# Layer 0's gate rows turned by way of DRAM and VectorE, two biases queued later, filler split between two places

## The chip, the core and the metric

The kernel runs on one core of a Trainium2 chip. The metric is device time in microseconds. TensorE (PE) multiplies matrices and loads their stationary operand (PEld), VectorE (DVE) and ScalarE (ACT) work on elements, GpSimd (POOL) does small elementwise work and issues indirect DMAs, SyncE (SP) issues most other DMAs. Each engine runs its own instructions in order and waits on semaphores.

## The reference

Two layers over N = 2708 rows of D = 256 features, in float32, with one adjacency matrix:

```python
def layernorm(x): return (x - mean(x)) / sqrt(var(x) + 1e-5)

# layer 0
n = layernorm(x)
s = where(adj > 0, (n @ Wq.T + bq) @ (n @ Wk.T + bk).T / 16, -9e15)
x = x + elu(softmax(s) @ (n @ Wv.T + bv))
n = layernorm(x)
# 8 experts, the best two per row, weights normalized over the two
xn = layernorm(n)
y_e = gelu((xn * ln_g[e] + ln_b[e]) @ W1[e] + b1[e]) @ W2[e] + b2[e]      # W1 256x1024
x = x + sum over the two of weight * y_e         # chosen by n @ Wr + br
# layer 1
h = layernorm(x) @ W_fc + b_fc
s = where(adj > 0, h @ w_att[:256] + (h @ w_att[256:]).T + b_att, -1e9)
x = x + softmax(s) @ h
n = layernorm(x)
x = x + sum over the best two of softmax weight * (gelu(n @ W1[e] + b1[e]) @ W2[e] + b2[e])   # W1 256x512
```

## The kernel before

**Tiles and blocks.** Rows are cut into 22 tiles of 128 (the last has 20 rows) and into six blocks of queries, five of four tiles and a last one of 148 rows. `layer0_attention` walks the blocks b and, inside each, the 22 key tiles k. At each k it makes scores (L545, PE), their exponential (L557, ACT), the product with the mask (L560, DVE; `p_last` in the last block), and, three steps later (LAG), the product with the values (L609, PE). The masks of the next block are made beside this: adjacency is loaded by SP (L394), compared (L411, DVE) and turned in 32 by 32 squares (L417, DVE). The experts' weights are copied into a packed layout in DRAM in the background, by SP (L1021 to L1034).

**Routing.** When a block ends, its four tiles are evicted (L634) and each becomes a generator, `finish`, that goes on into `Experts.route`. A `Line` starts a generator every third step (`gap`) and takes each running one a stage further at every k. In layer 0 a tile's route goes: statistics of the second layernorm (L251 to L257, the last on POOL); the row to `xd` in DRAM (L1120, SP), the normalized row `xn` and the twice normalized row for the experts (L261, DVE); the columns of `xn` for the gate by `to_columns`, which is two PE transposes (L274) and an ACT copy (L275) into `gT`; the gate product (L1156, PE) and its logits (L1160, DVE); the best two, their softmax (L1185, ACT), the place in the expert's region (L1188 to L1204); and two scatters of the row into `disp` (L1207, POOL). Once 16 tiles are routed, `begin` works out the first 24 slots (a slot is 128 rows of one expert) and fetches the first three, rows by SP (`fetch_rows`, L1388 to L1401: four quarters `xg` and the pair `who` of row number and weight), weights by POOL (`fetch_weights`, L1368, into a ring of four).

**Experts.** `slots` takes the slots one after the other. `turned` turns a slot's rows on DVE (L1436, then L1442 in layer 0); `up` makes the output bias times the row's weight (L1454 on DVE in layer 0, L1456 on ACT in layer 1) and the first product (L1463, PE) with gelu (L1471, ACT); `down` makes the second product (L1479, PE), the result `y` (L1485, DVE) and its scatter into `xd` (L1498 adds in layer 0, L1491 writes in layer 1). The products of neighbouring slots alternate on PE. SURE is 43 slots that there must be, SLOTS = 50 the most there can be. OFTEN = 45 slots run in a straight row; then every engine reads the number used (L1565), and each further slot stands in a nested `tc.If` (L1572). With these inputs layer 0 has 45 slots and layer 1 has 47. Weights are fetched three slots ahead, rows five, up to SLOTS.

**Layer 1's beginning.** `keys_and_values` puts PAUSE = 28 products that nobody reads on PE (`busy`, L914), loads the rows (L723) and norms them; the first use on PE is again a pair of transposes (L274).

**Order.** SP's order is the program's own throughout; so are those of PE, ACT and DVE in layer 1. In layer 0 the scheduler orders PE, ACT, DVE and POOL by its own estimates; `tc.issue_after(ins)` only says that an instruction comes behind `ins` on its engine.

Of the kernel before, what the change touches and what calls it, by code (L numbers as in the profile page):

```python
# [83 lines left out]

MASKS_AHEAD = 2

PAUSE = 28


FULL_AFTER = {14: 20, 16: 24}  # L90
# [2 lines left out]
SLOTS = (2 * N - E) // P + E  # L93
RING = 4

OFTEN = SURE + 2
AHEAD = 3
ROWS_AHEAD = 5
DROW = D + 2
# [5 lines left out]
def adj_ffn_kernel(ctx: ExitStack, tc: tile.TileContext, a: dict, out: bass.AP):  # L105
# [160 lines left out]
    def by_quarters(row):  # L266

        return row.rearrange("p (g c j) -> p g c j", g=GROUP, c=DC)

    def to_columns(dst, src, r):  # L270

        tp = misc.tile([P, GROUP, P], F32, name="misc")
        for c in range(DC):
            nc.tensor.transpose(tp[:, c, :r], src[:, c * P : (c + 1) * P], ident[:r, :r])  # L274
        nc.scalar.copy(dst, tp[:, :DC, :r])  # L275
# [77 lines left out]
    def layer0_attention(line):  # L353
        with ExitStack() as scope, ExitStack() as until_last:
# [18 lines left out]
            xin = {}  # L373

            def load_x(t):
                xin[t] = rows0.tile([P, D], F32, name="xin", bufs=9)
# [161 lines left out]
            def scores(b, k, g, apart, mT):  # L538
                b0, nb, ts_ = BLOCKS[b]
                kr, k0 = ROWS[k], k * P  # L540
                if k == NT - 1:
                    return tail_scores(b, g, apart, mT)
                ps = ps_s.tile([P, BN], F32, name="s")
                for c in range(DC):
                    nc.tensor.matmul(  # L545
                        ps[:kr, :nb], xnT[:, c, k0 : k0 + kr], g[:, c, :nb],
                        start=(c == 0), stop=(c == DC - 1 and k < KEYS),
                    )
                if k >= KEYS:
                    for j, t in enumerate(ts_):  # L550
                        r = ROWS[t]
                        nc.tensor.matmul(
                            ps[:kr, j * P : j * P + r], apart[:, j, :kr], minus_big[:, :r],
                            start=False, stop=(j == len(ts_) - 1),
                        )
                p = of_block(b, "p", [P, nb], F32, bufs=6)
                nc.scalar.activation(p[:kr, :nb], ps[:kr, :nb], AF.Exp, scale=1.0 / 16.0)  # L557
                mask = MASKS[b].of_key(mT, k)
                if k < KEYS:
                    nc.vector.scalar_tensor_tensor(  # L560
                        p, p, LARGEST, mask, op0=ALU.min, op1=ALU.mult
                    )
# [475 lines left out]
    class Experts:  # L1038
        def __init__(self, layer, hidden, packed_weights, w_gate, gate_bias, own_norm, xd, disp, early):
# [3 lines left out]
            self.seen = const.tile([P, E], BF16, name=f"seen{layer}")  # L1043
            nc.vector.memset(self.seen, 0.0)
            self.routed, self.begun, self.pads = 0, False, []
            self.written = []
            self.groups = [f"written{layer}", f"late{layer}", f"apart{layer}", f"after{layer}", f"rows{layer}"]
            self.early = early
# [55 lines left out]
        def route(self, t, x, logits=None):  # L1104
# [14 lines left out]
            if own_norm:  # L1119
                self.beside_early(nc.sync.dma_start(of_tile(xd, t), x[:r]))  # L1120

            if own_norm:
                xt = rows.tile([P, D], F32, name="xn", bufs=4)[:r]
                normed(xt, x[:r], mean, once)
                normed(by_quarters(rows2[:r, 0, :D]), in_chunks(x[:r]), mean, twice)
            else:
                row = normed(by_quarters(rows2[:r, 0, :D]), in_chunks(x[:r]), mean, once)
# [20 lines left out]
                )  # L1148
            lg = small.tile([P, E], F32, name="lg")
            if logits is None:  # L1150
                gT = routing.tile([P, DC, P], F32, name="gT", bufs=2)
                to_columns(gT[:, :, :r], xt, r)
                yield
                ps = misc.tile([P, GROUP, P], F32, name="misc").rearrange("p g n -> p (g n)")
                for c in range(DC):
                    nc.tensor.matmul(  # L1156
                        ps[:r, :E], gT[:, c, :r], w_gate[:, c, :],
                        start=(c == 0), stop=(c == DC - 1),
                    )
                nc.vector.tensor_add(lg[:r], ps[:r, :E], gate_bias[:r])  # L1160
            else:
                nc.vector.scalar_tensor_tensor(
                    lg[:r], logits, once, gate_bias[:r], op0=ALU.mult, op1=ALU.add
                )
# [201 lines left out]
        def fetch_weights(self, s, behind_add=None):  # L1366
            w, packed = self.ring[s % RING], self.packed_weights[0]
            start = nc.gpsimd.indirect_dma_start(  # L1368
                w, None, packed[:],
                bass.IndirectOffsetOnAxis(ap=self.weight_row[:, s : s + 1], axis=0),  # L1370
                bounds_check=E * P - 1, oob_is_err=False,
            )
            if behind_add is not None:
                tc.add_manual_dep(
                    start.ins, behind_add.ins.name,
                    mybir.DependencyInfo(
                        mybir.DependencyClass.Sync, mybir.DependencyReason.DATA
                    ),
                    reason="no sooner than the results",
                )  # L1380
            return w

        def fetch_rows(self, s):
# [41 lines left out]

        def slots(self, two, ps_mm, ps_acc, line):
            hidden, own_norm, xd = self.hidden, self.own_norm, self.xd
            _, hc, w2, b2, b1, ln, row = self.packed_weights

            def turned(s):  # L1430

                w, (xg, _) = self.weights[s], self.rows_[s]
                xe = two.tile([P, DC, P], F32, name="xe")
                raw = two.tile([P, DC, P], F32, name="xe_raw") if own_norm else xe
                with tc.issue_after(self.issued.ins) if own_norm and s < OFTEN else ExitStack():
                    nc.vector.transpose(  # L1436
                        raw.rearrange("p c (t i) -> p t c i", t=GROUP),
                        xg.rearrange("p t (c j) -> p t c j", c=DC),
                    )
# [9 lines left out]
            def up(w, xe, factor):  # L1449


                bias2 = two.tile([P, D], F32, name="bias2", bufs=2 if own_norm else 4)
                if own_norm:
                    nc.vector.tensor_scalar(bias2, w[:, b2:b1], factor, None, ALU.mult)  # L1454
# [21 lines left out]
            def down(s, w, who, hT, bias2, then):  # L1476
                ps = ps_acc.tile([P, D], F32, name="acc")
                for f in range(hc):
# [3 lines left out]
                    )  # L1482
                then()
                y = two.tile([P, D], F32, name="y", bufs=3)
                self.issued = nc.vector.scalar_tensor_tensor(  # L1485
                    y, ps, who[:, 1:2], bias2, op0=ALU.mult, op1=ALU.add
                )
                at = bass.IndirectOffsetOnAxis(ap=who.bitcast(I32)[:, 0:1], axis=0)
# [12 lines left out]
                if s < FULL_AFTER[self.early]:  # L1501
                    tc.declare_no_dep(start.ins, group=self.groups[3], reason="other rows of xd")
                    tc.add_to_no_dep_group(self.groups[2], start.ins)
                return start

            n = FULL_AFTER[self.early]
# [4 lines left out]
            def slot(s, s1):  # L1511
# [3 lines left out]
                    xe = turned(s)  # L1515

                after = turned(1) if s == 0 and not own_norm else None
                hT, bias2 = up(w, xe, who[:, 1:2])
                if s + 1 < s1 and not own_norm:
                    xe = after or turned(s + 1)  # L1520
                line.step()

                def fetch(behind_add=None):
# [30 lines left out]
            def in_a_row(s0, s1):  # L1554
# [6 lines left out]
                behind = None  # L1561


            in_a_row(0, OFTEN)
            used = nc.values_load(  # L1565
                self.used[0:1, 0:1], min_val=SURE, max_val=SLOTS,
                skip_runtime_bounds_check_because="a sum of rounded-up parts",
            )

            def others(s):  # L1570
                if s < SLOTS:
                    with tc.If(used > s):  # L1572
# [97 lines left out]
```

## Time and profile before

| | |
|---|---|
| median of 3 runs | 1231.23 us (1230.78 to 1231.45) |
| the profiled execution | 1228.5 us, its span 1226.7 us, mean granted TensorE clock 0.978 |
| TensorE matmul busy | 1150.6 us, 94% |
| VectorE, ScalarE, GpSimd busy | 565.7, 435.4, 421.3 us |
| layer 0: attention and experts | to about 510 us, and from there to 840 us |
| layer 1: attention and experts | from 847 us to about 1012 us, and from there to 1200 us |

A line of a group or of the timeline gives the engine, the line of the kernel, the operation, what it writes and reads, the shape and the count; in brackets stands the idle time before it and what ended it. A line of a stretch gives its length, the busy time of PE, PEld, DVE, ACT and POOL (each with its number of instructions), the granted clock, the share of the DMA engines and GB/s. A float32 product appears as two records, a transpose as one.

### The profile page before, as it was taken

To read this page: it belongs to the slowest core of one execution; us is meant where nothing else is said; L and a number is where in the kernel's file an instruction comes from. 1 tells how busy PE (TensorE), PEld (TensorE's weight loads), DVE (VectorE), ACT (ScalarE), POOL (GpSimd) and SP (SyncE) were. 2 spreads that over 40 slices of the span, in tenths; PEclk is the share of its full clock that TensorE was granted. 3 is DMA by queue.
4 is the path that set the end of the run, shared out by engine and by line. 5 is a ranking of instruction groups with operands and counts; after the bars stand their busy time and mean duration, and the time that the engine had idled before them with its cause. 6 is when DMAs were issued, how large, how long until landed. Compare 5 with 4: busy or idle time off the path is not lost. (4 is left out here: it accounts for less than half of the span.)

```text
span 1226.7 us, 20985 instructions
## 1 busy us (share of the span) xinstructions
PE 1150.6 (94%) x6528; PEld 928.7 (76%) x6528; DVE 565.7 (46%) x2147; ACT 435.4 (35%) x1254; POOL 421.3 (34%) x525
## 2 busy tenths in 40 slices
PE   8989999999998999789999999999999998999980
PEld 5656666666665675479999999997899977899880
DVE  5465663754546636352222222223866777422214
ACT  3222222222212212263233233232776757544330
POOL 3011020110211213053433343433654557655450
PEclk9999999999999999799999999999999999999996
DMA  9393973999988494538667966554001527655557
GB/s 205 59 178 69 197 163 101 211 197 235 227 175 202 104 211 193 175 63 258 168 183 207 344 155 176 128 169 105 8 1 41 206 58 202 186 155 141 143 184 278
DMA packets 206252, 198.17 MB, mean 162 GB/s; under 512 B 98027, under 2 KB 189636, under 8 KB 199992
## 3 DMA queue, kind: packets, MB, share of 16 engines
q1 hardware_dynamic: 178202, 110.45, 41.3%
q0 software_dynamic: 27040, 83.56, 21.6%
q10 hardware_dynamic: 894, 2.77, 0.6%
q8 instruction: 54, 0.88, 0.3%
q14 instruction: 62, 0.51, 0.1%
HBM read 263.92 MB, written 66.15 MB: 269 GB/s over the span
## 5 line engine op out<-in xcount | busy, mean ns | idle before, releaser
L1463 PEld LDWEIGHTS mm<-xe,ring 128*128 128x128 f32 x2192 | 261.9, 195 | 23.1 <-issue 7.0
L1463 PE MATMUL mm<-xe,ring 128*128 128x128 f32 x2192 | 267.5, 279 | 12.4 <-DMA ring<-L_ffn_packed,weight_row 4.7
L1479 PE MATMUL acc<-ring,hT 128*128 128x256 f32 x1096 | 255.0, 382 | 4.8 <-ACT hT L1471 4.8
L1471 ACT ACTIVATE hT<-mm,ring 128x128 f32<-128x128 f32 x548 | 156.8, 370 | 280.5 <-issue 156.9
L1479 PEld LDWEIGHTS acc<-ring,hT 128*128 128x128 f32 x1096 | 201.3, 191 | 29.8 <-ACT hT L1471 6.2
L609 PEld LDWEIGHTS acc<-v,p 128*128 128x128 f32 (+1 forms) x880 | 159.5, 190 | 65.7 <-issue 41.0
L609 PE MATMUL acc<-v,p 128*128 128x257 f32 (+1 forms) x880 | 204.1, 384 | 2.8 <-DVE p L560 1.8
L1485 DVE SCALAR_TENSOR_TENSOR y<-acc,who,bias 128x256 f32<-128x256 f32 x92 | 44.4, 483 | 345.6 <-PE acc L1479 337.6
L545 PE MATMUL s<-g,xnT 128*128 128x512 f32 x420 | 202.6, 602 | 0.0
L257 POOL TENSOR_TENSOR ln_rs<-ln_rs,minus_half 128x2 f32<-128x2 f32 x88 | 65.5, 748 | 266.0 <-DVE ln_rs L253 226.4
L1368 POOL DMA_INDIRECT ring<-L_ffn_packed,weight_row x98 | 103.6, 1057 | 145.7 <-PE acc L1479 107.1
L1207 POOL DMA_INDIRECT disp<-row,to x88 | 89.9, 1022 | 162.7 <-DVE to L1204 57.8
L854 PE MATMUL acc<-parts,m 128*128 128x266 f32 x924 | 127.7, 295 | 0.0
L557 ACT ACTIVATE p<-s 128x512 f32<-128x512 f32 x105 | 62.5, 596 | 180.5 <-PE s L545 146.1
L854 PEld LDWEIGHTS acc<-parts,m 128*128 128x128 f32 x924 | 118.3, 187 | 4.4 <-ACT raw L881 0.9
L545 PEld LDWEIGHTS s<-g,xnT 128*128 128x128 f32 x420 | 76.2, 192 | 53.7 <-issue 50.3
L560 DVE SCALAR_TENSOR_TENSOR p<-p,mT 128x512 f32<-128x512 f32 x100 | 68.3, 685 | 94.5 <-ACT p L557 94.4
L1498 POOL DMA_INDIRECT xd<-y,who x45 | 71.3, 1583 | 101.0 <-issue 59.2
L821 ACT CAST m<-mT 128x512 fp32r<-128x512 fp8e4 (+4 forms) x168 | 72.3, 475 | 11.2 <-PE acc L854 7.5
L1491 POOL DMA_INDIRECT xd<-y,who x47 | 47.0, 999 | 22.2 <-issue 11.6
L411 DVE TENSOR_SCALAR m_rows<-adj 128x512 fp8e4<-128x512 int32 (+1 forms) x105 | 42.1, 432 | 2.4 <-DMA adj<-in_adj_dram 2.4
L609 PE MATMUL acc<-v,p_last 128*128 128x257 f32 (+3 forms) x88 | 27.4, 413 | 8.8 <-DVE p_last L560 8.8
(251 smaller groups left out, 1040.8 us busy)
## 6 DMA issues: line engine op xcount, KB each, us to landing
adj<-in_adj_dram SPq DMA_DIRECT2D x100, 256.0 KB
L_ffn_packed<-in_L_ffn_W_dram SPq DMA_DIRECT2D x16, 1024.0 KB
xg<-disp SPq DMA_DIRECT2D x400, 32.0 KB
L_ffn_packed<-in_L_ffn_W_dram SPq DMA_DIRECT2D x16, 512.0 KB
neighbours<-mT SPq DMA_DIRECT2D x5, 1408.0 KB
mT<-neighbours SPq DMA_DIRECT2D x5, 1408.0 KB
xin<-in_x_dram SPq DMA_DIRECT2D x42, 128.0 KB
ring<-L_ffn_packed SPq DMA_DIRECT2D x4, 1154.0 KB
```

The source lines that it names most:

```text
L257: nc.gpsimd.tensor_tensor(rs[:r, 1], rs[:r, 0], minus_half[:r], ALU.pow)
L545: nc.tensor.matmul(ps[:kr, :nb], xnT[:, c, k0 : k0 + kr], g[:, c, :nb], start=(c == 0), stop=(c == DC - 1 and k < KEYS),)
L560: nc.vector.scalar_tensor_tensor(p, p, LARGEST, mask, op0=ALU.min, op1=ALU.mult)
L609: nc.tensor.matmul(accs[j][:r], p[keys, q0 : q0 + r], v[keys, k, :], start=(k == 0), stop=(k == NT - 1),)
L821: nc.scalar.copy(m[:, : q1 - q0], MASKS[b].of_key(mTs[b], k)[:, q0 - b * BN : q1 - b * BN],)
L854: nc.tensor.matmul(acc[:r], masks[t], parts[:, k, i], start=(k == 0 and i == 0), stop=False,)
L1207: nc.gpsimd.indirect_dma_start(disp[:], bass.IndirectOffsetOnAxis(ap=to[:r, j : j + 1], axis=0), rows2[:r, j], None,)
L1368: start = nc.gpsimd.indirect_dma_start(w, None, packed[:], bass.IndirectOffsetOnAxis(ap=self.weight_row[:, s : s + 1], axis=0), bounds_che ...
L1463: nc.tensor.matmul(ps[:, i, :], w[:, c * hidden + f * P : c * hidden + (f + 1) * P], xe[:, c, :], start=(c == 0), stop=(c == DC - 1),)
L1471: nc.scalar.activation(hT[:, f, :], ps[:, i, :], AF.Gelu, bias=w[:, b1 + f : b1 + f + 1])
L1479: nc.tensor.matmul(ps, hT[:, f, :], w[:, w2 + f * D : w2 + (f + 1) * D], start=(f == 0), stop=(f == hc - 1),)
L1498: start = nc.gpsimd.indirect_dma_start(xd[:], at, y, None, bounds_check=N - 1, oob_is_err=False, compute_op=ALU.add)
```

## The change

- The biases of layer 0's slots 0 and 1 are queued on DVE behind `self.issued`, which at that time is the first eviction copy of the last block.
- PAUSE goes from 28 to 12; 8 such products (BRIDGE) are put at the end of layer 0's row of slots.
- The row of slots is 45 long in layer 0, as before, and 47 in layer 1. Weights and rows are fetched up to that number and not beyond; a slot in a branch fetches its own. In layer 0 the number used is read behind the last scatter.
- For the 21 full tiles of layer 0, `xn` is written in feature quarters, stored to a scratch in DRAM, loaded back as four quarters on SP one stage later, and turned by one DVE transpose into `gT`, another stage later and behind the latest mask product or result. The tile of 20 rows keeps the PE transposes.

```diff
-PAUSE = 28
+PAUSE = 12
+BRIDGE = 8
...
-OFTEN = SURE + 2
...
+    def quarters(pool, name, src, bufs):
+
+        wide = D // GROUP
+        xq = pool.tile([P, GROUP, wide], F32, name=name, bufs=bufs)
+        for g in range(GROUP):
+            nc.sync.dma_start(
+                xq[g * QUARTER : (g + 1) * QUARTER],
+                src[:, g * wide : (g + 1) * wide].rearrange("(t i) e -> i t e", t=GROUP),
+            )
+        return xq
+
+    def turn(dst, xq):
+        return nc.vector.transpose(
+            dst.rearrange("p c (t i) -> p t c i", t=GROUP),
+            xq.rearrange("p t (c j) -> p t c j", c=DC),
+        )
...
# layer0_attention: mul_of = experts0.latest; scores():
-                    nc.vector.scalar_tensor_tensor(
+                    mul_of[0] = nc.vector.scalar_tensor_tensor(
                         p, p, LARGEST, mask, op0=ALU.min, op1=ALU.mult
                     )
...
# Experts.route:
+            turned = own_norm and r == P
             if own_norm:
                 xt = rows.tile([P, D], F32, name="xn", bufs=4)[:r]
-                normed(xt, x[:r], mean, once)
+                if turned:
+                    normed(by_quarters(xt), in_chunks(x), mean, once)
+                    scratch = dram.tile([P, D], F32, name=f"normed{t}")
+                    nc.sync.dma_start(scratch[:], xt)
+                else:
+                    normed(xt, x[:r], mean, once)
                 normed(by_quarters(rows2[:r, 0, :D]), in_chunks(x[:r]), mean, twice)
...
             if logits is None:
+                if turned:
+                    xq = quarters(rows0, "xq", scratch, 3)
+                    yield
                 gT = routing.tile([P, DC, P], F32, name="gT", bufs=2)
-                to_columns(gT[:, :, :r], xt, r)
+                if turned:
+                    with tc.issue_after(self.latest[0].ins) if self.latest[0] else ExitStack():
+                        turn(gT, xq)
+                else:
+                    to_columns(gT[:, :, :r], xt, r)
                 yield
...
# slots():
+            often = SURE + (2 if own_norm else 4)
...
                 if own_norm:
-                    nc.vector.tensor_scalar(bias2, w[:, b2:b1], factor, None, ALU.mult)
+                    with tc.issue_after(self.issued.ins) if gated else ExitStack():
+                        nc.vector.tensor_scalar(bias2, w[:, b2:b1], factor, None, ALU.mult)
...
-                self.issued = nc.vector.scalar_tensor_tensor(
+                self.issued = self.latest[0] = nc.vector.scalar_tensor_tensor(
                     y, ps, who[:, 1:2], bias2, op0=ALU.mult, op1=ALU.add
                 )
...
-                hT, bias2 = up(w, xe, who[:, 1:2])
+                hT, bias2 = up(w, xe, who[:, 1:2], own_norm and s < 2)
...
-                    if s + AHEAD < SLOTS and s + AHEAD == len(self.weights):
-                        self.weights.append(self.fetch_weights(s + AHEAD, behind_add))
+                    if len(self.weights) <= s + AHEAD < often:
+                        self.weights.append(self.fetch_weights(s + AHEAD))
                     for _ in range(2):
                         at = len(self.rows_)
-                        if at <= s + ROWS_AHEAD and at < (SLOTS if placed else n):
+                        if at <= s + ROWS_AHEAD and at < (often if placed else n):
                             self.rows_.append(self.fetch_rows(at))
...
-                elif own_norm and s == OFTEN - 1:
-
-                    added = down(*behind, lambda: None)
-                    fetch(added)
...
-            in_a_row(0, OFTEN)
-            used = nc.values_load(
-                self.used[0:1, 0:1], min_val=SURE, max_val=SLOTS,
-                skip_runtime_bounds_check_because="a sum of rounded-up parts",
-            )
+            in_a_row(0, often)
+            if own_norm:
+                idle = ps_mm.tile([P, GROUP, P], F32, name="mm").rearrange("p g n -> p (g n)")
+                for _ in range(BRIDGE):
+                    nc.tensor.matmul(idle[:, :D], ident, wfc[:, 0, :D], start=True, stop=True)
+            with tc.issue_after(self.last_start.ins) if own_norm else ExitStack():
+                used = nc.values_load(
+                    self.used[0:1, 0:1], min_val=SURE, max_val=SLOTS,
+                    skip_runtime_bounds_check_because="a sum of rounded-up parts",
+                )
 
             def others(s):
                 if s < SLOTS:
                     with tc.If(used > s):
+                        self.weights.append(self.fetch_weights(s))
+                        self.rows_.append(self.fetch_rows(s))
                         in_a_row(s, s + 1)
                         others(s + 1)
 
-            others(OFTEN)
+            others(often)
```

`to_columns`, `normed`, `by_quarters` and `in_chunks` stand as before; `turned` now calls `turn` for the same transpose it made itself.

More of the change, by code (lines that the diff above doesn't have):

```diff
@@ L372, in of_block @@
                 return pool.tile(shape, dtype, name=f"{name}_last", bufs=bufs)
-            xin = {}
+            xin, mul_of = {}, experts0.latest
             def load_x(t):
@@ L1045, in __init__ @@
             self.routed, self.begun, self.pads = 0, False, []
+            self.latest = [None]
             self.written = []
@@ L1364, in fill, with fetch_weights @@
                 yield
-        def fetch_weights(self, s, behind_add=None):
+        def fetch_weights(self, s):
             w, packed = self.ring[s % RING], self.packed_weights[0]
-            start = nc.gpsimd.indirect_dma_start(
+            nc.gpsimd.indirect_dma_start(
                 w, None, packed[:],
@@ L1372, in fetch_weights @@
             )
[L1373 to L1379, printed above, removed]
-                )
             return w
@@ L1434, in turned @@
                 raw = two.tile([P, DC, P], F32, name="xe_raw") if own_norm else xe
[L1435 to L1439, printed above, removed]
+                with tc.issue_after(self.issued.ins) if own_norm and s < often else ExitStack():
+                    turn(raw, xg)
                 if own_norm:
@@ L1447, in turned, with up @@
                 return xe
-            def up(w, xe, factor):
+            def up(w, xe, factor, gated):
                 bias2 = two.tile([P, D], F32, name="bias2", bufs=2 if own_norm else 4)
                 if own_norm:
-                    nc.vector.tensor_scalar(bias2, w[:, b2:b1], factor, None, ALU.mult)
+                    with tc.issue_after(self.issued.ins) if gated else ExitStack():
+                        nc.vector.tensor_scalar(bias2, w[:, b2:b1], factor, None, ALU.mult)
                 else:
@@ L1503, in down @@
                     tc.add_to_no_dep_group(self.groups[2], start.ins)
+                self.last_start = start
                 return start
@@ L1521, in slot, with fetch @@
                 line.step()
-                def fetch(behind_add=None):
+                def fetch():
                     for _ in range(2 if s + AHEAD < n else E):
@@ L1561, in in_a_row @@
                 behind = None
-            in_a_row(0, OFTEN)
-            used = nc.values_load(
-                self.used[0:1, 0:1], min_val=SURE, max_val=SLOTS,
-                skip_runtime_bounds_check_because="a sum of rounded-up parts",
-            )
+            in_a_row(0, often)
[8 more added lines that the diff above has]
+                )
             def others(s):
```

## The prediction

> **What bounds it now.** I read the page first: TensorE (PE) is busy nearly all the time, so a gain must come out of PE's own work or out of the few places where it stands still.
>
> ```profile
> PE 1150.6 (94%) x6528; PEld 928.7 (76%) x6528; DVE 565.7 (46%) x2147; ACT 435.4 (35%) x1254; POOL 421.3 (34%) x525
> ```
>
> Then busy time by stretch: layer 0's attention (to 510 us) and the experts after it. From 206 us PE is full and the DMA engines are full as well; in the last block, from 456 us, PE loses 9.2 of 54 us.
>
> ```profile
> 206.00:290.00 84.00, 84.00 (x336) 55.51 (x334) 44.63 (x164) 17.95 (x41) 12.84 (x21) 1.00 1.06 215
> ...
> 456.00:510.00 54.00, 44.80 (x224) 26.46 (x222) 24.53 (x124) 9.73 (x35) 12.99 (x18) 0.91 0.64 230
> ```
>
> The waits name that loss: VectorE (DVE) stands at slot 0's bias, whose rows have not landed, and the attention's mask product `p_last` is queued behind it.
>
> ```profile
> PE acc L609 <- DVE p_last L560: 8.8, 1, 8.8
> ...
> DVE bias L1454 <- DMA who<-disp: 13.0, 1, 13.0
> ```
>
> SyncE's (SP's) timeline shows why: slot 0's `who` is issued at 478.26 and the bias starts only at 497.57, 19.3 us later, while three weight gathers fill the DMA engines; rows for slot 2 take until 498.3, and only then come the row writes of tiles 17 to 19 (L1120).
>
> ```profile
> 478.26 0.40 SPq L1401 DMA_DIRECT2D who<-disp  x1
> ...
> 492.09 6.23 SPq L1395 DMA_DIRECT2D xg<-disp  x4
> ...
> 498.96 1.35 SPq L1120 DMA_DIRECT2D xd<-x  x3
> ```
>
> After the stall the granted clock is low for 5.5 us:
>
> ```profile
> 498.50:504.00 5.50, 5.47 (x14) 2.62 (x15) 1.53 (x7) 0.29 (x1) 2.11 (x4) 0.55 0.72 200
> ```
>
> Next the seam between the layers: last result (L1485), filler on PE (L914), a weight fetch that is not needed (L1368), the last scatter (L1498), the first row load, and layer 1's first transpose, which waits for the filler.
>
> ```profile
> 839.91 0.48 DVE L1485 SCALAR_TENSOR_TENSOR y<-acc,who,bias 128x256 f32<-128x256 f32 x1 [2.97 <-PE acc L1479]
> ...
> 841.49 12.32 PE L914 MATMUL acc<-wfc,ident 128*128 128x256 f32 x56 [1.62 <-DVEq L1572]
> 841.86 1.06 POOL L1368 DMA_INDIRECT ring<-L_ffn_packed,weight_row  x1 [3.08 <-PEq L1572]
> 843.22 1.57 POOL L1498 DMA_INDIRECT xd<-y,who  x1 [0.31 <-issue]
> ...
> 847.46 10.31 SPq L723 DMA_DIRECT2D kept<-xd  x22
> ...
> 853.65 0.38 PE L274 MATMUL misc<-ident,xn 128*128 128x128 f32 x2
> ```
>
> And layer 1's tail on PE: slots 45 and 46 run in branches, one after the other, with gaps.
>
> ```profile
> 1181.67 2.02 PE L1463 MATMUL mm<-xe,ring 128*128 128x128 f32 x16
> 1183.53 3.62 PE L1479 MATMUL acc<-ring,hT 128*128 128x256 f32 x16
> ...
> 1196.98 1.99 PE L1479 MATMUL acc<-ring,hT 128*128 128x256 f32 x8 [0.52 <-ACT hT L1471]
> ```
>
> **Part by part** (all against the profiled span of 1226.7 us).
>
> *Seam.* The last scatter has its row at 840.4 and needs the scatter before it to have landed; the wait on that ends at 841.1. Without L1368 and the register load ahead of it, it starts about 841.3 instead of 843.22, 1.9 us sooner, and with it the loads and the first `xn` (852.0 to 850.1). On PE 56 records took 12.32 us, 0.22 each. The bridge (16 records, 3.5 us) follows the last matmul at 839.87 directly, the branch costs about the 1.62 us it costs now, PAUSE 12 is 24 records, 5.3 us: PE is free at 850.3. The first transpose goes from 853.65 to 850.3: **-3.4** (-1.9 if filler is placed worse, -3.6 at best).
>
> Clock: the 1.62 us gap before L914 leaves the granted clock at 1.00 in the stretch after it, the 8.8 us stall brings 0.55; my gap stays at 1.6, so no price. The Trainium skill (TensorE: Matmul & The Clock Gate, Why this matters for your kernels) warns of idle gaps over about 3 us, after which the array runs at half clock; no row here lies between 1.6 and 8.8 us, and by the page a gap past 3 us would give back some 2 us as an estimate.
>
> *Tail.* Layer 1's straight row grows from 45 to 47 slots. A slot's period is 3.51 us (up starts at 1174.55 and 1178.07). From 1181.67, three ups and four downs back to back, as in the steady row, are 7 x 1.76 = 12.3, so PE ends at 1194.0 instead of 1198.97: **-4.9** (-3 if row loads come late). The unneeded fetches for slots 45 to 49 disappear from POOL and SP; they hid.
>
> *Transposes.* Each routed tile loses two on PE and a 371 ns copy on ScalarE. What PE gains is the step, not the 272 ns length:
>
> ```profile
> 407.80 0.42 PE L274 MATMUL misc<-ident,xn 128*128 128x128 f32 x2
> ...
> 408.05 1.88 PE L545 MATMUL s<-g,xnT 128*128 128x512 f32 x4
> ```
>
> 0.25 us per tile, 18 of the 21 full tiles inside the attention: **-4.5** (0 to -5.3). DVE gets 21 turns of 0.434 (L1436), 9.1 us in all; it is busy 5.3 tenths at 206 to 290, and PE takes a score's product three steps after it is made, about 10 us: 0.
>
> *The way through DRAM* adds on SP, per tile, one write and four loads, 105 issues of 0.32 to 0.6 us. The loads wait on SP for the write to land; behind them SP has adjacency, packing and, later, row loads. The turn sits in DVE's order, and the gate product L1156 in PE's, so both can hold up the attention. A 128 KB load with free engines is used 2.4 us after issue (847.46 to 849.85), the starved `who` 19.3 after; the round trip is two in series, 4.8 to 39 us. Hidden or not depends on where the scheduler puts the turn and L1156. In the present order it puts the mask turning late: adjacency loads issued from 224.5 are first used at 245.7, those from 264.7 at 302.9, and DVE waits 2.4 us in all at L411. It counts DMA on SP slower than it is, which leaves the turn late too. I take 0, the cover being those 20 to 38 us; uncovered, see the third rival.
>
> The Trainium skill (VectorE: DVE Perf Modes, Rules for kernel authors) speaks against the step: a 128x128 transpose belongs on TensorE if the result may be in PSUM. It also puts a DMA's fixed part near 2.0 us (DMA: Bandwidth & Descriptors, Anatomy of one DMA), which agrees with the 2.4 above. By that, two DMAs per tile, unhidden, would add 21 x 4 = 84 us; the sum above takes none of it.
>
> *Biases queued.* The biases of slots 0 and 1 go behind the first eviction copy (510.23 now), so the 8.8 us wait goes, and with it 0.45 x 5.5 = 2.5 us of low clock. Attention ends near 499; slot 0's `who` has landed at 497.5. I take **-10.5** (0 to -11.3). What could be late next is tile 17's turn: see the first rival.
>
> *Later routing.* If one more tile's softmax falls between gelus, it costs two table loads of 1283 ns: **+2.6** (0 to +7.7 for three). Three turns behind results in the expert stretch, where DVE's slack is a fraction of a us: **+0.9** (0 to +1.3).
>
> Sum: -3.4 -4.9 -4.5 -10.5 +2.6 +0.9 = -19.8. Span 1206.9; with the 1.8 around the span 1208.7; the median of the runs lies 2.7 above the profiled 1228.5: **1211.4 us**.
>
> **Rivals.**
> 1. *The stall moves to tile 17.* SP reaches its write at about 499, so its round trip ends at 504 to 505. If the scheduler put the turn inside the last block, DVE stands there as at the bias, and the -10.5 becomes 0 (up to +5, as 505 is later than 497.6): 1222, to 1227. For: the bias itself was placed 13 us too early, so its estimates can be short when gathers run. Against: tile 18's `xn` stands after the attention although its statistics were ready near 483, so a queue behind DMAs is counted as slow. Chance 0.22.
> 2. *Nothing moves by the DRAM way.* PE's 4.5 us are lost again to small waits of L1156 and the routing moves: 1216 to 1218, chance 0.1.
> 3. *Slower: L1156 waits in PE's order for the round trip.* Place: tiles 4 to 15, where the DMA share is 1.02 to 1.06 and SP stands in queue. The point where it decides is 20 us over 12 tiles, 1.7 us a tile; at 4.8 us a tile, one free round trip, it is +58; I price it at 3 us, +36: 1247. For: DMA is saturated there, every engine is in order. Against: the 20 to 38 us above. Chance 0.18.
>
> **How the numbers follow.** Forecast 0.5, rivals 0.22, 0.1, 0.18. The low end takes every best bound: -3.6 -5 -5.3 -11.3 = -25.2, 1206, and 3 us for an order that I can't see: 1203. The high end takes rival 1 whole and half of rival 3: 1240. 0.2% is 2.5 us, about what a measurement of this kernel can tell from no change. Slower by that: rival 3 (0.18). Same: a mild rival 3 or rival 1 at its worst (0.06). Faster: 0.76.
>
> **What would show it.** Right: no PE wait on `p_last` near 9 us; granted clock 1.00 through the last block; last scatter of layer 0 less than 2 us after its `y`; first layer 1 transpose some 10 us after that `y` instead of 13; ups and downs without gaps to the last slot; DVE waits at the new turn of under 5 us in all. Wrong: PE idle at L1156 or DVE idle at the turn with `xq` as releaser, in the blocks from 206 to 456 (rival 3) or once before the first expert (rival 1).

## Result, and the profile after

The changed kernel takes **1264.9 us** (median; 1264.0 to 1271.8) against 1231.3 us of the kernel before in the same comparison: ratio **1.028, interval 1.024 to 1.032**, slower by 34 us. The forecast was 1211.4, range to 1240: wrong in sign. The profiled execution took 1265.5 us, its span 1263.5.

First the page of the kernel after, the line of the engines' busy times. PE has less to do, 58 records fewer, and is still busy 2.6 us longer, over a span 37 us longer.

```profile
PE 1153.2 (91%) x6470; PEld 926.5 (73%) x6470; DVE 576.1 (46%) x2168; ACT 429.1 (34%) x1235; POOL 413.7 (33%) x519
```

Then busy time by stretch (length, busy us of PE, PEld, DVE, ACT and POOL, granted clock, DMA share, GB/s), the same two stretches as before:

```profile
206.00:290.00 84.00, 75.23 (x255) 46.87 (x254) 40.66 (x138) 15.71 (x33) 9.51 (x17) 0.94 0.90 200
...
456.00:510.00 54.00, 52.03 (x255) 34.71 (x254) 31.25 (x135) 11.02 (x35) 12.34 (x20) 0.97 0.63 162
```

The loss is where the kernel before was full: 8.8 us of PE in the first of them. The last block gained, but now ends at 530.1 us (510.7 before). The waits on PE name what is late:

```profile
PE mm L1485 <- DMA xg<-disp: 14.7, 1, 14.7
PE misc L1187 <- DVE gT L282: 10.9, 5, 3.5
PE misc L1219 <- DVE sel L1214: 6.3, 7, 1.1
...
PE misc L235 <- ACT gT L292: 5.2, 1, 5.2
```

The 8.8 us at `p_last` are gone. In their place stand the first slot's rows (L1485 is the first product of the experts), the gate product waiting for the new turn (L1187, L1156 before), the rank that follows it (L1219), and `fold_gate` (L235).

The timeline shows one of these places, the end of the third block:

```profile
299.07 0.51 PE L1187 MATMUL misc<-wr,gT 128*128 128x8 f32 x4
299.62 0.17 DVE L1191 TENSOR_TENSOR lg<-misc,L_ffn_br_b 128x8 f32<-128x8 f32 x1 [8.09 <-PE misc L1187]
...
300.72 0.17 PE L1219 MATMUL misc<-sel,before 128*128 128x8 bf16 x1 [1.14 <-DVE sel L1214]
...
303.52 0.61 DVE L434 STREAM_TRANSPOSE mT<-m_rows 128x128 int32<-128x128 int32 x2
...
303.99 0.40 DVE L282 STREAM_TRANSPOSE gT<-xq 128x256 f32<-128x256 f32 x1
304.45 1.02 PE L1187 MATMUL misc<-wr,gT 128*128 128x8 f32 x4 [3.53 <-DVE gT L282]
```

Two tiles' gate products stand next to each other in PE's order, with no score between them. VectorE waits 8.1 us for the first; only behind its logits, and behind mask work, comes the next tile's turn; for that PE waits 3.5 us. That tile's quarters had landed at 279.1, 25 us sooner; SP had issued their loads from 267.22 on:

```profile
267.22 8.28 SPq L275 DMA_DIRECT2D xq<-normed  x4
```

For tiles 4 to 11 the trace has 12 to 39 us between the last quarter's landing and the turn. Inside the gap the granted clock falls: it is 1.00 to 301.4, 0.50 from there to 311.7.

```profile
300.00:304.00 4.00, 0.19 (x2) 0.10 (x1) 3.79 (x20) 0.30 (x2) 1.30 (x2) 0.68 0.91 294
304.00:308.00 4.00, 2.41 (x8) 1.82 (x9) 2.50 (x16) 0.30 (x2) 0.65 (x1) 0.50 1.14 215
308.00:312.00 4.00, 4.00 (x6) 1.54 (x5) 0.00 (x0) 0.69 (x1) 1.92 (x2) 0.54 0.87 166
```

What runs there, most at 1061 ns a product instead of 592, is L546: the queries of the next block, without which no score of it can start. First their line after, then before (L529), where a score follows at once:

```profile
306.67 6.16 PE L546 MATMUL misc<-xnT,aT 128*128 128x512 f32 x8
```

```profile
268.21 3.60 PE L529 MATMUL misc<-xnT,aT 128*128 128x512 f32 x8
271.64 1.88 PE L545 MATMUL s<-g,xnT 128*128 128x512 f32 x4
```

From 120 to 560 us the granted clock is 0.94, against 0.98 before; this is part of why PE is busy longer with fewer records. In PE's order the queries now stand behind the last score of their block in four of five blocks; in the kernel before that was so in one, and in three they stood about four rounds of keys sooner.

SP's timeline for the first slots: `who` of slot 0 at 519.41 (478.26 before), and tile 17's row write behind twelve row loads, at 545.30.

```profile
519.41 0.46 SPq L1424 DMA_DIRECT2D who<-disp  x1
520.38 5.27 SPq L1418 DMA_DIRECT2D xg<-disp  x4
...
536.40 8.30 SPq L1418 DMA_DIRECT2D xg<-disp  x4
...
545.30 0.42 SPq L1138 DMA_DIRECT2D xd<-x  x1
```

The seam: the last scatter is 0.8 us behind its `y` (3.3 before), SP's loads 6.6 us (7.55 before), the first transposes 11.9 us (13.7 before).

```profile
876.74 0.48 DVE L1507 SCALAR_TENSOR_TENSOR y<-acc,who,bias 128x256 f32<-128x256 f32 x1 [6.54 <-PE acc L1501]
877.50 1.55 POOL L1520 DMA_INDIRECT xd<-y,who  x1 [5.48 <-DVE y L1507]
...
888.67 0.44 PE L291 MATMUL misc<-ident,xn 128*128 128x128 f32 x2 [0.53 <-DVE xn L261]
```

The tail on PE, straight now, waits for weights between the last slots:

```profile
1224.65 2.02 PE L1485 MATMUL mm<-xe,ring 128*128 128x128 f32 x16 [0.50 <-DMA ring<-L_ffn_packed,weight_row]
...
1229.45 2.02 PE L1485 MATMUL mm<-xe,ring 128*128 128x128 f32 x16 [1.05 <-DMA ring<-L_ffn_packed,weight_row]
```

From the layer-1 part's first transpose to its last result it is 346.8 us, 345.8 before. So nearly all of the loss is there by the first product of the experts, which starts 33 us later than before (544.8 against 511.8). From there on the results of the experts come 26 to 41 us later than before, the last 36.

### The profile page after: what moved, and what is told of

It is laid out like the page before. It is cut to its first block, busy times and chain, and to the rows that moved or that the text cites. A ratio compares the mean times of both kernels' runs of the same rounds, so it can differ in the third digit from the quotient of the medians.

```text
span 1263.5 us, 20873 instructions
## 1 busy us (share of the span) xinstructions
PE 1153.2 (91%) x6470; PEld 926.5 (73%) x6470; DVE 576.1 (46%) x2168; ACT 429.1 (34%) x1235; POOL 413.7 (33%) x519
## 5 line engine op out<-in xcount | busy, mean ns | idle before, releaser
L1485 PE MATMUL mm<-xe,ring 128*128 128x128 f32 x2192 | 266.7, 279 | 30.5 <-DMA xg<-disp 14.7
L1485 PEld LDWEIGHTS mm<-xe,ring 128*128 128x128 f32 x2192 | 262.4, 195 | 41.1 <-issue 25.3
L626 PE MATMUL acc<-v,p 128*128 128x257 f32 (+1 forms) x880 | 207.2, 386 | 3.7 <-ACT p L574 2.3
L1399 POOL DMA_INDIRECT ring<-L_ffn_packed,weight_row x92 | 97.3, 1057 | 120.4 <-PE acc L1501 78.0
L434 DVE STREAM_TRANSPOSE mT<-m_rows 128x128 int32<-128x128 int32 x100 | 33.1, 394 | 0.1
```

What stands on the lines that cost most here:

```text
L626: nc.tensor.matmul(accs[j][:r], p[keys, q0 : q0 + r], v[keys, k, :], start=(k == 0), stop=(k == NT - 1),)
L1399: nc.gpsimd.indirect_dma_start(w, None, packed[:], bass.IndirectOffsetOnAxis(ap=self.weight_row[:, s : s + 1], axis=0), bounds_check=E * P ...
L1485: nc.tensor.matmul(ps[:, i, :], w[:, c * hidden + f * P : c * hidden + (f + 1) * P], xe[:, c, :], start=(c == 0), stop=(c == DC - 1),)
```

## Experiments

The medians of the kernel before were 1227.9 us in the comparison of the first four runs, 1228.4 in the next four, 1229.1 and 1234.4 in the last two; so ratios are compared, and "us" of a difference is its ratio times 1231. "Attention ends" is the last product with the values in the profiled execution.

| run | time | ratio to before, interval | attention ends | first product of the experts |
|---|---|---|---|---|
| after | 1264.9 | 1.028 (1.024 to 1.032) | 530.1 | 544.8 |
| before | 1231.3 | 1 | 510.7 | 511.8 |
| no way | 1211.9 | 0.988 (0.985 to 0.990) | 499.9 | 500.8 |
| way only | 1268.9 | 1.033 (1.030 to 1.035) | 546.4 | 547.2 |
| trip unread | 1228.2 | 1.000 (0.998 to 1.001) | 506.1 | 519.9 |
| late by hand | 1215.0 | 0.989 (0.987 to 0.991) | 504.5 | 505.5 |
| queries first | 1254.0 | 1.021 (1.018 to 1.024) | 517.8 | 531.6 |
| turn later | 1246.7 | 1.014 (1.011 to 1.017) | 519.8 | 534.1 |
| one stage | 1215.0 | 0.989 (0.986 to 0.991) | 498.1 | 505.4 |
| no way, queries first | 1211.5 | 0.985 (0.982 to 0.988) | 499.9 | 500.9 |
| pinned 3 | 1257.1 | 1.022 (1.019 to 1.024) | 547.1 | 548.1 |
| pinned 2 | 1258.6 | 1.022 (1.020 to 1.025) | 551.4 | 552.3 |
| no landing wait | 1224.3 | 0.996 (0.994 to 0.998) | 505.6 | 514.9 |
| biases only | 1214.5 | 0.988 (0.985 to 0.990) | 499.3 | 500.3 |
| pinned, tiles 0 to 15 | 1236.6 | 1.002 (1.000 to 1.003) | 521.5 | 523.7 |
| way, tiles 0 to 15 | 1258.1 | 1.020 (1.018 to 1.021) | 532.0 | 545.5 |
| way, tiles 16 to 20 | 1226.7 | 0.993 (0.991 to 0.995) | 497.9 | 500.9 |
| trip on GpSimd | 1290.5 | 1.046 (1.044 to 1.048) | 557.9 | 558.9 |

### The way through DRAM taken out, and put in alone

```diff
-            turned = own_norm and r == P
+            turned = False
```

> The changed kernel with PE's transposes back for all tiles (no scratch, no quarters, no turn, no extra stage); biases, filler, straight rows and fetches as changed. In PE's order the gate products stand where they stood before (after 26, 29, 32, 35 rounds of keys, and so on). Theory A (the way through DRAM is the loss, because turn and gate product stand late in the order): 1209 to 1218 us, no PE wait at the gate product over 0.5 us. Theory B (SP's 105 more issues and their traffic are the loss): the same 1209 to 1218. Theory C (the loss is in the other parts, such as the later fetches or the queued biases): 1240 us or more.

1211.9 us, and no wait at the gate product. Theory C falls: the way through DRAM is the whole loss, 50 us (1.028 less 0.988), and the rest of the change is a gain of 15.

The opposite edit, the kernel before with `quarters`, `turn`, the scratch and the stage and nothing else:

> The kernel before with the way through DRAM alone. A and B: the seam is worth 1.8 us in the trace, the tail about 0, and the biases' gain is lost behind the later rows, so 1264 to 1272 us, with the first slot waiting for its rows some 10 to 15 us. C: 1229 to 1238 us.

1268.9 us, as expected. The first slot's late rows show at another place: VectorE stands 18.6 us at the first bias, ahead of the attention's last mask work, and PE 14.4 us at the products behind it, since this kernel does not queue the bias later.

### Transfers without the turn, lateness without transfers

In the first, the quarters are stored and loaded, and PE's transposes make `gT`:

```diff
-                    normed(by_quarters(xt), in_chunks(x), mean, once)
+                    normed(xt, x[:r], mean, once)
...
-                if turned:
-                    with tc.issue_after(self.latest[0].ins) if self.latest[0] else ExitStack():
-                        turn(gT, xq)
-                else:
+                if True:
                     to_columns(gT[:, :, :r], xt, r)
```

> The changed kernel with the scratch write, the four quarter loads and the extra stage kept, but nobody reads the quarters: PE's transposes make the columns. In PE's order the gate products stand one round of keys later than before (27, 30, 33, 36). A: within 5 us of the kernel without the way, 1210 to 1222 us. B: near the changed kernel, 1250 to 1268 us, SP still waiting some 40 us for the writes to land.

In the second, the kernel without the way gets ten idle stages:

```diff
-            turned = own_norm and r == P
+            turned = False
...
+                    if own_norm:
+                        for _ in range(10):
+                            yield
                     to_columns(gT[:, :, :r], xt, r)
```

> The kernel without the way through DRAM, with ten more stages put ahead of PE's transposes in layer 0's route: no scratch, no DMA more, only lateness. In PE's order the gate products stand 9 to 10 rounds later than before (36, 39, 42, 45; at the ends of the blocks 64, 64 and 86, 86). A: most of the loss comes back without any transfer, 1240 to 1265 us. B: 1209 to 1222 us.

The first, 1228.2 us, lies in neither theory's range: transfers and stage cost 16 us, more than A gave them and far less than B. The second, 1215.0, lies in B's range, and theory A falls with it: gate products ten rounds late cost nothing that the intervals tell (0.989 against 0.988). With unread quarters the loss is paid at the first slot's rows, where the kernel without the way has no such wait, and SP stands until writes have landed:

```profile
PE mm L1482 <- DMA xg<-disp: 13.8, 1, 13.8
```

```profile
SPq L275 <- DMA normed<-xn: 46.7, 14, 8.5
```

The row writes of tiles 4 to 7 (L1138) leave at 227.5, 244.5, 260.7 and 276.2 there, at 228.0, 240.8, 251.7 and 259.4 without the way: SP needs 16 us a tile instead of 10.5, and the program starts a tile every three rounds, 10.4 us. In the changed kernel they leave at 225.1, 243.5, 260.6 and 276.8. At these tiles SP is behind the program's pace, and the lag lasts: tile 15's row write leaves at 448.5 us with unread quarters and at 429.6 without the way, slot 0's row loads at 491.1 and 475.6.

### The extra stage, and SP's standing

One idle stage instead of ten, no transfers:

> The kernel without the way through DRAM, with one more stage ahead of PE's transposes: the stages of the run in which nobody read the quarters, without its transfers. Theory S (the 16 us of that run come from the stage, which sets the table of the first slots behind another tile's routing, so that slot 0's rows land late): 1222 to 1230 us with a wait for the first rows of 10 us or more. Theory T (they come from the transfers): 1210 to 1215 us, no such wait.

1215.0 us: theory T, at the edge of its range; PE stands 1.9 us before the first product, not 10. From here to the run with unread quarters, which has the same stages, the transfers cost 13 us (0.989 to 1.000).

Unread quarters again, but loaded from an older scratch, so that SP need not wait for a landing:

```diff
+                    earlier = self.stored[max(0, len(self.stored) - 5)]
...
-                    xq = quarters(rows0, "xq", scratch, 3)
+                    xq = quarters(rows0, "xq", earlier, 3)
```

> The run with unread quarters, its quarters now loaded from the scratch of the tile four before, so that SP need not stand until a write has landed: same issues, same bytes, same order on PE. Theory W (SP's standing, 47 us in 14 waits, made that run 13 us slower than the one with the stage alone): 1214 to 1220 us. Theory I (its issues and bytes did): 1224 to 1230 us.

1224.3 us, in theory I's range: 4.5 less by ratio, with intervals that touch. If that holds, a third of the 13 goes with SP's standing. But SP is hardly sooner for it: its pace at tiles 4 to 7 is 15 us, tile 15's row write leaves at 448.1 us and slot 0's loads at 490.0. So most of SP's lag is its issues, their bytes, and its waits for earlier DMAs of its own (16 us at L275 between 206 and 400 us); it stays open how these share it.

### Why late is dear only in the changed kernel

The gate product, `fold_gate` and the queries take turns in a PSUM pool of two banks (the ring), in the order of the program. Lateness by hand moves the gate product behind the queries in the program too. The scheduler's lateness does not: the queries, traced at round 16 of a block, must wait for banks that late gate products of earlier rounds hold. Two edits free them. One traces the queries at round 5:

```diff
-                    if k == NT - 6 and b + 1 < len(BLOCKS):
+                    if k == 5 and b + 1 < len(BLOCKS):
```

> The changed kernel, way through DRAM and all, but each next block's queries are traced at round 5 of a block instead of round 16, ahead of the block's gate products in the two-bank ring of PSUM that both use. The gate products stand as late in PE's order as in the changed kernel (28, 33.5, 39, 44; 58.5, 64, 64, 67.5), the queries at 25, 47, 69, 91 instead of 44, 64, 86, 108. Theory E (late gate products hold the next block's queries in the ring, and PE has no scores left at a block's end): attention ends 20 us sooner or more, near 505 to 512 us, and the time is 1232 to 1247 us. Theory D (the gate products themselves wait for the late turn on VectorE, wherever the queries stand): saves under 8 us, 1256 to 1265 us.

The other puts the turn eight more stages later:

```diff
                     xq = quarters(rows0, "xq", scratch, 3)
-                    yield
+                    for _ in range(8):
+                        yield
```

> The changed kernel with the turn eight stages later in the program, about where the scheduler put it of itself; the gate products stand as late or later (34, 37, 40, 44; 59, 64, 64, 67.5), but the queries, traced before them now, stand at 36, 59, 86, 103.5. E: later is faster: attention ends near 510 to 518 us, 1235 to 1250 us. D: 1260 to 1275 us.

1254.0 and 1246.7 us: 9 and 18 less by ratio. The first lies between the two ranges, and its interval touches that of the changed kernel; the second lies in E's range. Making it later made it faster, which theory D alone can't give, and both edits put the queries sooner in PE's order. So the ring is one part, on the strength of the second edit above all. But attention ends at 518 to 520 in both, and E wanted 505 to 512 of the first. D is at work too, as the waits on PE with the queries first say: the same two turns per block, as late as ever.

```profile
PE misc L1187 <- DVE gT L282: 12.7, 6, 3.6
PE misc L1219 <- DVE sel L1214: 8.1, 7, 2.1
```

The early queries in the kernel without the way, where they were held up in one block:

> The kernel without the way through DRAM, with the queries at round 5. Before, PE waited 3 us for the fourth block's rest behind queries at a block's end (84). E: queries at 64 and 86 at the latest, a gain of up to 4 us, 1207 to 1212 us. D: no difference, 1210 to 1214 us.

1211.5 us; by ratio 0.985 against 0.988, with intervals that overlap. It decides nothing.

### The turn forced to its place

The mask product and the score that are traced some rounds later are queued behind a tile's turn and gate product:

```diff
+        def behind(self, those, late):
+            stack = ExitStack()
+            while those and those[0][0] + late <= self.rounds:
+                stack.enter_context(tc.issue_after(those.pop(0)[1].ins))
+            return stack
...
+                with experts0.behind(experts0.gates, 3):
                     for c in range(DC):
...
+                    with experts0.behind(experts0.turns, 3):
                         mul_of[0] = nc.vector.scalar_tensor_tensor(
```

> The changed kernel with the turn and the gate product pinned: the mask product traced three rounds of keys after a tile's turn comes behind that turn on VectorE, and the score three rounds after its gate product behind that product on PE. Nothing else differs. The gate products then stand at 54, 57, 60, 63 and 76, 79, 82, 85 (rounds of values done) in place of 56, 64, 64, 66 and 84, 86, 86, 88. Theory P (the data have long landed and only the place in the order costs): no bunches at the blocks' ends, attention ends near 506 us as in the run with unread quarters, and the time is 1218 to 1232 us. Theory Q (the trip itself is too slow to be used this early): waits at the turn for the quarters, 1245 us or more.

> The same with two rounds instead of three: gate products at 53, 56, 59, 62 and 75, 78, 81, 84. P: within 4 us of the one with three, 1216 to 1232 us. Q: the trip needs 9 to 18 us from the write's issue to the last quarter in the trace of the changed kernel and gets some 14, so VectorE waits for quarters and it is slower than with three by 5 us or more.

Both stay above 1255, and P falls for the kernel as a whole. Nor are two rounds slower than three by the 5 us that theory Q asked for (1.022 both). Of the wait on PE with three rounds, 25.3 us are one wait, at a tile of the last block: its write stands behind twelve row loads on SP, as the write at 545.30 in the changed kernel.

```profile
PE misc L1198 <- DVE gT L282: 44.9, 8, 25.3
```

So the next runs leave the last block's tiles to PE's transposes, with the pin and without:

```diff
-            turned = own_norm and r == P
+            turned = own_norm and t < 16
```

> Pinned three rounds behind as before, but tiles 16 to 20 go by PE's transposes. Theory P2 (the pin frees the blocks' ends, and the 25.3 us wait of PE in the last block, where a tile's write stands behind twelve row loads on SP, hid it): attention ends near 520 us or sooner, 1222 to 1235 us. Theory Q2 (the trip is too slow in all blocks): 1240 us or more.

> The changed kernel with the way through DRAM for tiles 0 to 15 alone, nothing pinned. If the loss splits by place as the trace says (30 us by the end of attention, most of it by tile 15, and 14 us at the first slot's rows from tiles 16 to 20): attention ends near 525 us, little wait for the first rows, 1240 to 1250 us. If the wait for the first rows comes from the late sixteenth tile: 1252 to 1262 us.

> The way through DRAM for tiles 16 to 20 alone. By place: attention ends near 500 us, PE waits 5 to 15 us for the first slot's rows, 1215 to 1227 us. If the first rows are late only because tile 15 is routed late: 1210 to 1215 us.

The last has the condition the other way round. By ratio, the way for tiles 0 to 15 costs 39 us, for tiles 16 to 20 it costs 7, for all 50. The wait for the first slot's rows stays (13.4 us) when tiles 16 to 20 don't take the way, and is 3.1 when only they do: it comes from the late sixteenth tile, on which the table of the slots depends. My expectation by place had that the wrong way round, though the 1226.7 us lie in its range. The 7 us of that run come behind the first product, which starts at 500.9 us as without the way (500.8): by the sixth result of the experts it is 6 us later. What makes them stays open.

With the pin the 39 become 17 (1.002 less 0.988); in microseconds that run lies between the ranges, just above P2's, in a comparison in which the kernel before was 6 us above the others. So, by this difference, 22 us are the place that the scheduler chose, ring included, and 17 remain when turn and product stand early. What they are, the waits of VectorE and PE between 120 and 520 us show:

```profile
DVE gT L282 <- DMA xq<-normed: 30.6, 6, 9.4
```

```profile
PE misc L1198 <- DVE gT L282: 23.1, 7, 7.2
```

Now the quarters really are not there. At tiles 5, 6, 9 and 10 the turn starts within 0.2 us of the landing, and there SP reaches the write of the scratch 14 to 18 us after that of the tile before.

### Another queue

```diff
-                    nc.sync.dma_start(scratch[:], xt)
+                    nc.gpsimd.dma_start(scratch[:], xt)
...
-            nc.sync.dma_start(
+            nc.gpsimd.dma_start(
                 xq[g * QUARTER : (g + 1) * QUARTER],
```

> The changed kernel, all 21 tiles by way of DRAM, but the scratch write and the four loads are issued by GpSimd in place of SP. In PE's order the gate products now stand one round behind those of the kernel before (27, 30, 33, 36; 49, 52, 55, 58), so the scheduler's own estimate put them late for SP's queue alone. Theory R (SP's queue is the cause: its estimate, and its standing): 1212 to 1226 us. Theory Q2 (the trip is too slow through any queue, or GpSimd's other work, statistics and scatters, now stands behind the write's landing): VectorE and PE wait in the order for the turn, 1235 us or more.

1290.5 us, the slowest of all; R falls. VectorE's waits:

```profile
DVE gT L282 <- DMA xq<-normed: 54.3, 6, 14.4
```

In the scheduler's order the gate product stands one round behind where it stood with PE's transposes; the trip takes 11 to 19 us from the write's issue at tiles 4 to 11. So its order is too late for the trip on SP (12 to 39 us behind the landing) and too early for the trip on GpSimd, and in the early place the engines wait for the quarters on both queues.

### The biases alone

> The kernel before with the two biases queued behind the first eviction copy and nothing else. The prediction's term was -10.5 us. The trace of the kernel without the way through DRAM has attention ending 10.8 us sooner than before and slot 16's result 14.9 us sooner, so 1214 to 1218 us against 1228 in that comparison; if the shorter fetches and not the biases brought part of it, 1219 to 1223 us.

1214.5 us, ratio 0.988: the same as all of the change but the way.

## Why the prediction was wrong, point by point

- **The way through DRAM, taken at 0: the step that failed.** It costs 50 us. I had argued that the scheduler counts SP's DMAs as slow, so that the turn would come late enough to be covered by 20 to 38 us. The turn did come 12 to 39 us after the landing at tiles 4 to 11. But I read "late" as "covered" and didn't ask who stands behind a late turn: its tile's gate product, through the two banks the next block's queries, through the sixteenth tile the first slots' rows. And I counted SP's 105 issues without asking whether SP still keeps the pace of 10.4 us a tile; it needs 16 there, and 15 in the run in which it needn't wait for a landing.
- **The transposes, -4.5.** No run separates them from the rest of the way; whatever they gave is in the 50 us.
- **Rival 3 (slower, 1247, chance 0.18)** had the sign and the place, L1187 in PE's order between 206 and 456 us, and not the mechanism: only 10.9 us of PE's waits are at L1187, for turns whose data had landed. Its own mechanism, waiting for the round trip, is what the pinned runs show (PE 23.1 us with tiles 0 to 15).
- **Rival 1.** SP reaches tile 17's write behind the row loads, as it says, at 545 us. Unpinned, the attention does not wait for it; pinned, it is the 25.3 us.
- **Rival 2** (PE's 4.5 us lost to small waits, 1216 to 1218) lies far below the result.
- **The biases, -10.5.** The mechanism was right and the size short: the run with them alone gains 15 us by ratio. Attention ends 11.4 us sooner in its trace than before, and some 4 us more come by slot 16; no run says what gives these 4.
- **The seam, -3.4, and the tail, -4.9.** Mis-sized: together they are lost in the intervals (the biases alone equal all of the rest). In the trace without the way the first transposes are 1.3 us closer to the last `y`, and the scatter starts 1.5 us sooner; but SP's loads start 7.8 us after that `y` (7.55 before), and PE stands 2.7 us for `xn`. I had taken the loads to follow the scatter's start. In the tail the gaps were those of the branches, but the weights come no faster: PE waits 10.1 us for them in layer 1 there, 4.7 before, and the stretch from the first transpose to the last result is 0.7 us shorter instead of 4.9.
- **Later routing and the turns, +2.6 and +0.9.** The stage alone, 3 us in the medians, lies within the intervals.
- **The rules of the Trainium skill.** "VectorE: DVE Perf Modes" (Rules for kernel authors), which wants a 128x128 transpose on TensorE where PSUM will do, spoke against the step, and the runs agree: 0.988 with PE's transposes, 1.028 without. I had set it aside because VectorE had time; what it lacked was the data's way. "TensorE: Matmul & The Clock Gate" (Why this matters for your kernels) says that an idle gap of over about 3 us brings half clock. The traces agree only roughly. In the changed kernel PE stood 1.1 us from 299.6 and 3.5 us from 300.9, and the clock was 0.50 from 301.4, inside the second gap. And the prediction's "no row here lies between 1.6 and 8.8 us" overlooked rows of the kernel before: PE stood 3.0 us from 372.2 (L552) and 2.1 to 2.4 us from 527.8, 1002.3, 1037.3 and 1135.4, and each time the clock was 0.50 for 3.4 us, from 2 to 5 us after the gap's start. A gap of 2.15 us in the changed kernel, from 1038.1, cost no clock. So no sharp bound comes out of these traces. The seam, with gaps of at most 1.3 us, kept 1.00. The 2.0 us that the prediction took from "DMA: Bandwidth & Descriptors" (Anatomy of one DMA) are fitted there on DMAs that GpSimd issues; its estimate of 84 us from them, for trips wholly unhidden, stands against 50 us measured for the whole way.

## What to carry to other kernels

A step that is moved behind a transfer is covered only if nothing behind it is waited for: list who takes the next buffer of every pool that it holds, in program order, and what is traced late but needed early. A queue that issues in program order has a pace per tile; before adding a write and a load that depends on it, compare that pace, with the new issues and the standing, to the pace of the loop. The kernel without the way through DRAM beats both kernels here: 1211.9 us, 1.0 to 1.5% faster than before, and nearly all of it comes from two biases queued later.

## What the runs showed of the hardware

- A store to DRAM and a load of the same row, both on SP, took 8 to 18 us from the write's issue to the last quarter's landing in the full blocks (tiles 4 to 11; DMA share 0.90 from 206 to 290 us, 0.83 from there to 375), and 5 us at tile 0 (share 0.16). The write alone landed after 1.8 us at tile 0 and after 2.4 to 8 us at tiles 4 to 11.
- The wait for that landing is spent on the queue: SP issues nothing meanwhile, 43.4 us in 13 waits in the changed kernel. "DMA: Bandwidth & Descriptors" (Anatomy of one DMA) of the Trainium skill says that a DMA's wait happens on the issuing sequencer; these waits agree.
- The same trip issued by GpSimd was no shorter: 11 to 19 us at the same tiles.
